# A graph attention kernel on one core: the same operations, ordered by a plan with other sizes and paces of transfers and longer bank copies

## The chip, the core and the metric

One core of a Trainium2 chip. The metric is device time of one execution, in microseconds (us): the median of several runs, on the same data. The engines: PE (TensorE, with PEld for its weight loads), DVE (VectorE), ACT (ScalarE), POOL (GpSimd) and SP (SyncE, which here only issues transfers). SP's transfers make one queue, POOL's another.

## The reference

Input: `x` of 32 x 512 x 512 (32 graphs, 512 nodes, 512 features, f32) and `adj` of 32 x 512 x 512. Per graph, a layer norm and a relu, then two graph attention layers, and the input is added:

```
def gat_layer(x, mask, W, a_src, a_dst, bias, concat):
    xl = (x @ W).reshape(B, N, H, F)
    asrc = einsum('bnhf,hf->bnh', xl, a_src); adst = einsum('bnhf,hf->bnh', xl, a_dst)
    e = leaky_relu(asrc[:, :, None, :] + adst[:, None, :, :], 0.2)
    attn = softmax(where(mask[..., None], e, -1e9), axis=1)
    out = einsum('bsdh,bshf->bdhf', attn, xl)      # heads side by side, or their mean
    return out + bias
h = relu(layernorm(x)); mask = (adj > 0) | eye(N)
h = elu(gat_layer(h, mask, W1, ..., concat=True))      # 4 heads of 256
x = x + gat_layer(h, mask, W2, ..., concat=False)      # 1 head of 512
```

## The kernel before

The kernel writes no loop of instructions in the order in which they run. `tile_gat` adds *jobs* to a `Program`: each has an engine, a cost in us, the keys that it reads and writes, and a function that emits its instructions. A DMA job has also a *size*: the time in us for which the plan takes it to occupy its queue. After all jobs are added, `Program.order` simulates the engines with these costs and so decides each engine's order, and `emit` writes the instructions out in that order. So every instruction stands where the plan put it, and each engine runs its own list in order, waiting by semaphores for data and for buffers that are still read.

How the plan chooses: among the jobs of an engine that are ready, it takes the one with the smallest rank. The ranks come from the table `PLACES` (2374 entries in hundredths of a us): one entry for each job up to the end of the first round (1144), for each of the 470 jobs of a round, and for each job from the last round on (760); a round's entries are used for all rounds between, shifted by the TensorE time of a round (84.5 us by the plan's costs). Transfers are modelled as two wires, SP's and POOL's: a transfer starts `DMA_LEAD` after its issue, lasts its size, and is seen by its readers `DMA_TAIL` later. If both wires are busy, `SHARED` gives the pace of each as a share of its full speed; before, it has two cases, a transposing transfer on SP (of size `TURN`) or any other.

Work is staged so that three graphs are in hand. Round i (lines 1599 to 1650) does, in the order in which the jobs are added:
- the first attention layer's gather of graph i+1, heads 0 and 1 (L1607, `gather1`) and 2 and 3 (L1623), with the softmax numerators of heads 2 and 3 (L1608, L1609, `second`);
- the second layer's scores and numerators of graph i (L1610 `second_layer`, L1611), its gather with the residual (L1632 `residual`, L1633 `gather2`) and the store;
- the first projection of graph i+2 in two halves (L1617 and L1625, `project1`), its masks (L1614 `masks`), its scores (L1619 and L1628 `columns`; L1620, L1621, L1629 and L1630 `first`) and the numerators of heads 0 and 1 (L1626, L1627 `second`);
- load and norm of graph i+3 (L1635, L1636), the second projection of graph i+1 (L1647 `project2`), and the transposing of graph i+3 (L1650 `norm_turn`).

The products use a scheme of seven instead of eight block products (`sevens`): a product's result in a PSUM bank is copied or added out by ACT or DVE (`put`, tile `xl` for the first projection), and one result of each seven is also copied to a second bank by ACT (`FORK`, L1051, `mm<-mm` in the profile); `HALF` is the cost of the halved bank copies of the inner scheme (`step`), `BIAS` that of the gathers' results, `PUT` that of the second gather's.

The scores reach all partitions by way of DRAM (`spread`, L821 on): DVE transposes a small block (L830), SP stores it (`das<-as` or `drr<-rr`, 4 KB), and SP reads it back, repeated over 128 partitions (`as<-das` or `rr<-drr`, 512 KB, for one row pair 256 KB). ACT reads `as` in `first` (`l<-as,z`), DVE reads `rr` in `second` (`p<-rr,z`). The mask is added to the numerators by POOL's transfers (`p<-dm`, two of 512 KB for each head, accumulating), and ACT takes the Exp of the sum (`p<-p,z`).

All instructions are emitted through helpers, so the profile shows ACT's at L498, DVE's at L501, SP's copies at L504, POOL's transfers at L509 and TensorE's at L515, and tells them apart by tiles.

Of the kernel before, what the change touches and what calls it, by code (L numbers as in the profile page):

```python
# [19 lines left out]
P = 128  # L20
# [24 lines left out]
class Banks(Slots):  # L45
# [176 lines left out]
class Program:  # L222
# [9 lines left out]
    DMA_LEAD, DMA_TAIL, AHEAD = {"SP": 0.6, "POOL": 0.75}, {'SP': 1.2, 'POOL': 1.2}, 3.5  # L232
    ALONE = {"SP": 1.0, "POOL": 1.0}
    SHARED = {0: {"SP": 0.44, "POOL": 0.62}, 1: {"SP": 0.3, "POOL": 0.62}}
    TURN = 0.95
    ENGINES = "PE", "ACT", "DVE", "POOL", "SP"

    def __init__(self):
# [44 lines left out]
    def order(self):  # L283
        jobs, rank = self.jobs, self.ranks()
        n = len(jobs)
# [1406 lines left out]
```

## Time and profile before

| | |
|---|---|
| median of 3 runs | 2817.1 us (2813.84 to 2825.34) |
| the profiled execution | 2829.0 us, its span 2827.2 us |
| instructions of the span | 42339 |
| granted TensorE clock, mean | 0.999 |
| transfers | 502.12 MB, mean 178 GB/s |
| share of 16 DMA engines: SP's queue, POOL's queue | 43.1%, 24.8% |
| transfers issued by SP, by POOL | 1296, 318 |

How to read it: the profile is one execution. A group's row gives engine, operation, tiles (written <- read), shape and count, then the busy time, the mean of one in ns, and the idle time of the engine ahead of them with what ended it. A row of a timeline gives the start and the length in us, and in brackets the idle time ahead and its releaser. A row of the waits gives who waited for whom, then the total in us, how often, and the longest. A row of the windows gives the stretch, its length, and the busy time of PE, PEld, DVE, ACT and POOL with their instructions, then the granted clock, the DMA share and GB/s. A wait for several semaphores is put down to the one that came last by the profile.

### The profile page before, as it was taken

To read this page: it belongs to the slowest core of one execution; us is meant where nothing else is said; L and a number is where in the kernel's file an instruction comes from. 1 tells how busy PE (TensorE), PEld (TensorE's weight loads), DVE (VectorE), ACT (ScalarE), POOL (GpSimd) and SP (SyncE) were. 2 spreads that over 40 slices of the span, in tenths; PEclk is the share of its full clock that TensorE was granted. 3 is DMA by queue.
4 is the path that set the end of the run, shared out by engine and by line. 5 is a ranking of instruction groups with operands and counts; after the bars stand their busy time and mean duration, and the time that the engine had idled before them with its cause. 6 is when DMAs were issued, how large, how long until landed. Compare 5 with 4: busy or idle time off the path is not lost.

```text
span 2827.2 us, 42339 instructions
## 1 busy us (share of the span) xinstructions
PE 2766.5 (98%) x12924; PEld 2369.7 (84%) x12924; DVE 2544.8 (90%) x6732; ACT 2223.8 (79%) x4907; POOL 320.0 (11%) x356
## 2 busy tenths in 40 slices
PE   7999999999999999999999999999999999999999
PEld 6688888888888888888888888888888888888877
DVE  8999989999989999999999898899998998989996
ACT  5968888778787787887787877878878788778873
POOL 0110111101111111111011110111110111101110
PEclk9999999999999999999999999999999999999999
DMA  8756866666766767667676667776666766668663
GB/s 232 177 155 165 207 168 179 178 178 180 188 168 172 183 172 197 178 170 194 165 198 172 180 171 182 177 187 183 172 188 163 197 173 170 190 165 198 159 170 104
DMA packets 375863, 502.12 MB, mean 178 GB/s; under 512 B 222804, under 2 KB 227668, under 8 KB 375636
## 3 DMA queue, kind: packets, MB, share of 16 engines
q1 hardware_dynamic: 329844, 332.68, 43.1%
q0 software_dynamic: 45792, 166.74, 24.8%
q8 instruction: 102, 1.67, 0.2%
q14 instruction: 125, 1.02, 0.1%
HBM read 316.41 MB, written 51.31 MB: 130 GB/s over the span
## 4 chain that ended last, share of the span: by engine, by line
PE 37%; DMA 20%; ACT 19%; DVE 15%; issue 3%; SPq 1%; DVEq 0%; ACTq 0%; POOLq 0%
PE mm L515 37%; ACT l L498 10%; DMA as<-das 7%; DVE p L501 6%; DMA rr<-drr 5%; DMA drr<-rr 4%; ACT p L498 3%; DMA x<-in_x_dram 2%; DVE l L501 2%; DVE t L501 2%; ACT xl L498 2%; DVE h L501 1%; ACT mm L498 1%; ACT x L498 1%; DVE xl L501 1%
## 5 line engine op out<-in xcount | busy, mean ns | idle before, releaser
L515 PE MATMUL mm<-w_sb,hs 128*128 128x257 f32 (+3 forms) x2908 | 668.2, 368 | 18.3 <-ACT mm L498 11.8
L515 PEld LDWEIGHTS mm<-w_sb,hs 128*128 128x128 f32 x2908 | 532.4, 190 | 98.0 <-ACT mm L498 16.6
L509 POOL DMA_DIRECT2D p<-dm x314 | 273.8, 902 | 2306.4 <-DVE p L501 1375.1
L515 PE MATMUL mm<-w_sb,ht 128*128 128x258 f32 x2112 | 520.1, 383 | 11.8 <-DVE xl L501 11.6
L515 PE MATMUL mm<-p,xl 128*128 128x258 f32 (+2 forms) x1984 | 511.2, 385 | 2.5 <-ACT h L498 1.1
L515 PE MATMUL mm<-w_sb,h 128*128 128x257 f32 x2056 | 483.1, 380 | 3.5 <-ACT xl L498 2.4
L501 DVE SCALAR_TENSOR_TENSOR p<-rr,z 128x512 f32<-128x512 f32 (+1 forms) x636 | 444.7, 745 | 36.1 <-DMA rr<-drr 36.0
L498 ACT ACTIVATE p<-p,z 128x512 f32<-128x512 f32 (+1 forms) x636 | 425.6, 712 | 43.0 <-DMA p<-dm 30.1
L498 ACT ACTIVATE l<-as,z 128x512 f32<-128x512 f32 x516 | 355.9, 714 | 127.4 <-DMA as<-das 126.9
L515 PEld LDWEIGHTS mm<-w_sb,ht 128*128 128x128 f32 x2112 | 390.6, 191 | 72.5 <-DVE xl L501 20.8
L515 PEld LDWEIGHTS mm<-w_sb,h 128*128 128x128 f32 x2056 | 387.9, 189 | 65.9 <-ACT xl L498 7.1
L515 PEld LDWEIGHTS mm<-p,xl 128*128 128x128 f32 x1984 | 367.3, 190 | 71.9 <-DVE p L501 7.8
L498 ACT ACTIVATE l<-l,low 128x512 f32<-128x512 f32 x516 | 368.6, 718 | 15.1 <-DVE low L501 14.6
L501 DVE CUSTOM_DVE_ANT_1 l<-l,mt 128x512 f32<-128x512 f32 x516 | 349.4, 687 | 23.8 <-ACT l L498 19.6
L498 ACT ACTIVATE xl<-mm 128x258 f32<-128x258 f32 (+2 forms) x748 | 272.0, 377 | 101.0 <-PE mm L515 99.0
L498 ACT ACTIVATE mm<-mm 128x257 f32<-128x257 f32 (+2 forms) x498 | 171.7, 345 | 150.5 <-PE mm L515 150.4
L498 ACT ACTIVATE h<-mm,b_sb 128x256 f32<-128x256 f32 (+1 forms) x504 | 225.3, 472 | 57.3 <-PE mm L515 55.5
L515 PE MATMUL mm<-t,hs 128*128 128x258 f32 (+1 forms) x992 | 246.5, 380 | 0.5 <-DVE t L501 0.5
L515 PEld LDWEIGHTS mm<-t,hs 128*128 128x128 f32 x992 | 186.1, 190 | 30.1 <-DVE xl L501 3.7
L515 PE MATMUL mm<-xl,p 128*128 128x258 f32 (+2 forms) x752 | 195.1, 389 | 3.2 <-DVE h L501 2.1
L498 ACT ACTIVATE xr<-h 128x512 f32<-128x512 f32 x256 | 157.8, 624 | 47.9 <-DVE h L501 45.6
L501 DVE TENSOR_TENSOR xl<-xl,mm 128x258 f32<-128x258 f32 x372 | 153.3, 419 | 29.8 <-PE mm L515 27.9
(137 smaller groups left out, 3727.7 us busy)
## 6 DMA issues: line engine op xcount, KB each, us to landing
p<-dm POOLq DMA_DIRECT2D x314, 512.0 KB, 5.5
rr<-drr SPq DMA_DIRECT2D x159, 512.0 KB
x<-in_x_dram SPq DMA_DIRECT2D x129, 256.0 KB
adj<-in_adj_dram SPq DMA_DIRECT2D x128, 256.0 KB
as<-das SPq DMA_DIRECT2D x64, 512.0 KB
t<-in_x_dram SPq DMA_DIRECT2D x124, 256.0 KB
out_dram<-t SPq DMA_DIRECT2D x124, 256.0 KB
dm<-m SPq DMA_DIRECT2D x64, 256.0 KB
```

Of the source, the lines that this page charges most:

```text
L498: prog.add("ACT", cost, reads, writes, lambda: nc.scalar.activation(*a, **k))
L501: prog.add("DVE", cost, reads, writes, lambda: f(*a, **k))
L509: lambda: nc.gpsimd.dma_start(to, at, accum_op=OP.add), size,
L515: f(*a, **k)
```

## The change

Every job stays, with the same keys, instructions and buffers. Changed are numbers that the plan uses: the table `PLACES` (all 2374 entries), the sizes and paces of the transfers, and some costs of ACT's bank copies. `SHARED` is now looked up by the size of the transfer that SP has under way, with (0.4, 0.6) for sizes that are not listed. Since the plan decides the order, the order of the instructions on PE, DVE, ACT, SP and POOL changes all over, and with it the order in which buffers are taken. The changed kernel's lines stand one lower than those named here.

```
-    DMA_LEAD, DMA_TAIL, AHEAD = {"SP": 0.6, "POOL": 0.75}, {'SP': 1.2, 'POOL': 1.2}, 3.5
-    ALONE = {"SP": 1.0, "POOL": 1.0}
-    SHARED = {0: {"SP": 0.44, "POOL": 0.62}, 1: {"SP": 0.3, "POOL": 0.62}}
-    TURN = 0.95
+    DMA_LEAD, DMA_TAIL, AHEAD = {"SP": 0.45, "POOL": 0.42}, {'SP': 1.2, 'POOL': 1.15}, 3.5
+    SHARED = {0.93: (0.31, 0.7), 0.77: (0.43, 0.71), 2.32: (0.75, 0.31), 1.16: (0.75, 0.31), 1.25: (0.35, 0.57)}
...
-            speed = self.ALONE
+            speed = dict.fromkeys(wires, 1.0)
             if len(busy) == 2:
-                speed = self.SHARED[jobs[wires["SP"][0][0]][4] == self.TURN]
+                speed["SP"], speed["POOL"] = self.SHARED.get(jobs[wires["SP"][0][0]][4], (0.4, 0.6))
...
+    XLOAD, STORE, MASKS, TURN, MASK_OUT, SMALL_ONE = 0.93, 0.77, 2.35, 1.25, 0.8, 0.1
+    ROWS = {4: 1.16, 8: 2.32}
     COPY, ADD, TINY = 0.266, 0.335, 0.08
-    BIAS, FORK, HALF, PUT = 0.37, 0.27, 0.17, 0.4
+    BIAS, FORK, HALF, PUT = 0.365, 0.303, 0.197, 0.394
```

The sizes that are used at the transfers:

| transfer | before | after |
|---|---|---|
| loads of x (also of the residual) and adj, 256 KB | 0.8 | 0.93 |
| loads of W1 | 0.9 | 0.93 |
| store of the output, 256 KB | 0.65 | 0.77 |
| the mask's add, `p<-dm`, 512 KB | 2.3 | 2.35 |
| the mask to DRAM, `dm<-m` | 1.0 | 0.8 |
| transposing transfers | 0.95 | 1.25 |
| the small store of `spread` | 0.2 | 0.1 |
| the repeated read of `spread`, 4 or 8 rows | 0.96, 1.92 | 1.16, 2.32 |

More of the change, by code (lines that the diff above doesn't have):

```diff
@@ L595, in weights1 @@
                     dma(
-                        0.9, (), [("w1", ix, k)], w1_sb[:, ix, k, :, 2:],
+                        XLOAD, (), [("w1", ix, k)], w1_sb[:, ix, k, :, 2:],
                         w1[row : row + P, :].rearrange("p (j c f) -> p c j f", j=H // 2, c=2)[:, c],
@@ L701, in load @@
             xt = xt[:, :D]
-            dma(0.8, (), [xk], xt, x[b, t * P : (t + 1) * P, :])
+            dma(XLOAD, (), [xk], xt, x[b, t * P : (t + 1) * P, :])
             XT[b].append((xk, xt))
@@ L713, in masks @@
                 row = (2 * g + t) * P
-                dma(0.8, (), [ak], a, adj[b, row : row + P, :])
+                dma(XLOAD, (), [ak], a, adj[b, row : row + P, :])
                 dve(
@@ L727, in masks @@
             dma(
-                1.0, every, [mk + (g,)],
+                MASK_OUT, every, [mk + (g,)],
                 md[:, 2 * g : 2 * g + 2].rearrange("p t n -> p (t n)"), m.rearrange("p t n -> p (t n)"),
@@ L736, in masks @@
                 ),
-                prog.TURN,
+                TURN,
             )
@@ L795, in norm_turn @@
                 ),
-                prog.TURN,
+                TURN,
             )
@@ L834, in spread @@
             dma(
-                0.2, [ok], [dk], dr[:k].rearrange("k (b j) -> b k j", j=32),
+                SMALL_ONE, [ok], [dk], dr[:k].rearrange("k (b j) -> b k j", j=32),
                 bass.AP(
@@ L841, in spread @@
             dma(
-                0.24 * rows * n, [dk], [ok], o[:, :rows, : n * P],
+                ROWS[rows * n], [dk], [ok], o[:, :rows, : n * P],
                 bass.AP(tensor=dr.tensor, offset=dr.offset, ap=[[0, P], [n * P, rows], [1, n * P]]),
@@ L961, in second @@
                         accumulate(
-                            2.3, keys + [mk + (us[0] // 2,)], keys,
+                            MASKS, keys + [mk + (us[0] // 2,)], keys,
                             *(t[:, us[0] : us[-1] + 1].rearrange("p t n -> p (t n)") for t in (p, md)),
@@ L1427, in residual @@
             halves = [xk, xk + (0,), xk + (1,)]
-            dma(0.8, [x2_key(b, 0, 0)], halves, xr, x[b, d * P : (d + 1) * P, :])
+            dma(XLOAD, [x2_key(b, 0, 0)], halves, xr, x[b, d * P : (d + 1) * P, :])
             XR[b].append((places[d], xk, xr))
@@ L1484, in put @@
                 upper[u[0]] = -1
-                dma(0.65, [xk, xk + (0,), xk + (1,)], (), out[b, d * P : (d + 1) * P, :], xt)
+                dma(STORE, [xk, xk + (0,), xk + (1,)], (), out[b, d * P : (d + 1) * P, :], xt)
                 place.give(xk)
@@ L1511, in gather2_plain @@
             dve(0.6, [bk, xk], [xk], nc.vector.tensor_add, xr, ps, xr)
-            dma(0.65, [xk], (), out[b, d * P : (d + 1) * P, :], xr)
+            dma(STORE, [xk], (), out[b, d * P : (d + 1) * P, :], xr)
             banks.give(bk)
```

309 rows, old and new, of the table PLACES are left out of this document.

## The prediction

> **What bounds the kernel now.** I read the page's first part, then busy time in three stretches, then TensorE's own waits in the long middle one.
>
> ```profile
> PE 2766.5 (98%) x12924; PEld 2369.7 (84%) x12924; DVE 2544.8 (90%) x6732; ACT 2223.8 (79%) x4907; POOL 320.0 (11%) x356
> ```
> ```profile
> 0.00:87.00 87.00, 70.42 (x316) 57.27 (x317) 74.54 (x294) 52.95 (x121) 8.17 (x14) 1.00 0.79 225
> 87.00:2720.00 2633.00, 2596.88 (x12198) 2235.08 (x12198) 2393.37 (x6251) 2119.61 (x4674) 304.07 (x333) 1.00 0.69 178
> 2720.00:2827.20 107.20, 99.21 (x412) 77.36 (x410) 76.88 (x191) 51.23 (x114) 7.79 (x9) 0.98 0.47 134
> ```
> ```profile
> PE mm L515 <- DVE xl L501: 12.4, 18, 1.4
> PE mm L515 <- ACT mm L498: 11.8, 17, 2.2
> PE mm L515 <- DVE hs L501: 3.5, 6, 1.1
> PE mm L515 <- DVE mm L501: 3.3, 3, 1.7
> PE mm L515 <- ACT xl L498: 2.4, 4, 1.0
> ```
> ```profile
> L515 PE MATMUL mm<-w_sb,ht 128*128 128x258 f32 x2112 | 520.1, 383 | 11.8 <-DVE xl L501 11.6
> ```
> ```profile
> 1542.81 1.69 PE L515 MATMUL mm<-w_sb,hs 128*128 128x258 f32 x7
> ```
>
> TensorE is the bound; in the middle (about 29 rounds) it idles 2633.0 - 2596.9 = 36.1 us. The change keeps every instruction, so only waiting can go. A wait costs a little more than its row shows, because a matmul's record outlasts the start of the next: one is recorded with 383 ns, and 7 in a row take 1.69 us, so starts are (1.69 - 0.38) / 6 = 0.218 us apart and each gap hides about 0.16. (A product of four such matmuls is so 0.87 us of TensorE, one of eight 1.74, one of two half-wide ones 0.22; I use these below.) With that: **A**, waits on DVE's xl, 12.4 + 18 x 0.16 = 15.3 us; **B**, waits on ACT's copies into a bank (FORK), 11.8 + 17 x 0.16 = 14.5; **C**, the three other rows, 9.2 + 13 x 0.16 = 11.3. Together 41.1 us is what the middle can give back, 1.5%. One round shows A and B:
>
> ```profile
> 1513.00:1600.40 87.40, 85.61 (x404) 73.78 (x404) 78.80 (x208) 69.29 (x154) 10.08 (x11) 1.00 0.68 177
> ```
> ```profile
> 1529.03 0.33 SPq L504 DMA_DIRECT2D x<-in_x_dram  x1
> 1529.47 0.37 SPq L504 DMA_DIRECT2D adj<-in_adj_dram  x1
> 1531.08 0.54 SPq L504 DMA_DIRECT2D drr<-rr  x1
> 1531.67 0.51 SPq L504 DMA_DIRECT2D das<-as  x1
> 1532.29 0.66 SPq L504 DMA_DIRECT2D adj<-in_adj_dram  x1
> 1537.34 0.33 SPq L504 DMA_DIRECT2D rr<-drr  x1
> ```
> ```profile
> 1530.85 0.21 DVE L501 STREAM_TRANSPOSE rr<-low 128x32 f32<-128x32 f32 x1
> ...
> 1538.24 0.69 DVE L501 TENSOR_TENSOR ht<-ht 128x512 f32<-128x512 f32 x1
> 1538.84 0.30 DVE L501 TENSOR_TENSOR mm<-mm,f 128x129 f32<-128x129 f32 x1
> ...
> 1539.73 0.30 DVE L501 TENSOR_TENSOR mm<-mm,f 128x129 f32<-128x129 f32 x1
> 1541.87 1.42 DVE L501 SCALAR_TENSOR_TENSOR p<-rr,z 128x512 f32<-128x512 f32 x2 [1.84 <-DMA rr<-drr]
> ```
> ```profile
> 1545.08 0.42 DVE L501 TENSOR_TENSOR xl<-xl,mm 128x258 f32<-128x258 f32 x1
> ...
> 1545.55 1.79 PE L515 MATMUL mm<-w_sb,ht 128*128 128x258 f32 x7 [1.06 <-DVE xl L501]
> ```
>
> This is A. The small row drr (made by first of L1630) is put on SP behind an x load and an adjacency load; the copy rr<-drr that needs it can be issued only at 1537.34, 6.3 us later, behind yet another adjacency load. DVE waits 1.84 us for it, its put of xl ends late at 1545.5, and TensorE loses 1.06 us. DVE is not the bound, but its queue hands the late landing on.
>
> ```profile
> 1553.15 0.52 SPq L504 DMA_DIRECT2D das<-as  x1
> 1553.77 0.39 SPq L504 DMA_DIRECT2D rr<-drr  x1
> 1555.37 0.33 SPq L504 DMA_DIRECT2D t<-in_x_dram  x1
> 1555.80 0.38 SPq L504 DMA_DIRECT2D as<-das  x1
> ```
> ```profile
> 1561.65 1.95 ACT L498 ACTIVATE l<-as,z 128x512 f32<-128x512 f32 x3 [1.05 <-DMA as<-das]
> ```
> ```profile
> 1564.44 1.79 PE L515 MATMUL mm<-w_sb,hs 128*128 128x258 f32 x7 [0.66 <-ACT mm L498]
> ```
>
> This is B: the copy as<-das is issued behind a residual load, ACT stands 1.05 us before its first use, three of these and one more instruction stand ahead of the bank copy, and TensorE waits for that copy. The round's idle time, 87.40 - 85.61 = 1.79 us, is nearly these two gaps, 1.06 + 0.66.
>
> **The change, part by part.** The new sizes and paces move no work by themselves; through the table they give another order, which I read from the built programs. Of one round in the middle:
>
> *A.* On SP the order before is adj, x, adj, drr, das, adj, rr, as, adj; after it is adj, drr, adj, x, das, rr, as, adj, adj. So drr passes two loads and the third adjacency load no longer stands before the copies. On DVE 26 instructions stood between the transpose (1530.85) and the first use of rr, 9.0 us (1531.06 to 1540.03); after it is 33. The net addition is four 512-wide subtractions (0.60 each, as from 1538.24 to 1538.84: the next begins 0.09 before a record of 0.69 ends), an add on rr (1.42 / 2 = 0.7), a 256-wide one (0.42 - 0.09 = 0.33) and two small ones (0.21 - 0.09 = 0.12 each, by the transpose), less one 512-wide statistic (0.60): +3.1 us. The lateness of 1.84 becomes at least 1.2 us of slack (3.1 - 1.84). The issue of rr itself comes 0 to 3.6 us sooner (drr to rr took 6.26 here; das to as, with a copy and a load in between, 2.65); at both ends the wait is gone. The PE product that waits moves four products back too (0.87 each), but the put it needs moves back on DVE as well, so I count nothing for that. A gives back 15.3 us at most; DVE had other small lags in front of the put, and if those alone cause half of it, 8. I take **14**, near the upper end, because the row names the DMA and both edits strike at it.
>
> *B.* On SP the residual load (256 KB) goes behind as<-das. From 1553.77 to 1561.65 a 512 KB, a 256 KB and a 512 KB transfer took 7.9 us; the load's share is 0 us if it was hidden and 7.9 x 256 / 1280 = 1.6 if they run in turn. The transpose that feeds das comes 0 to 1.84 us sooner when A's wait is gone. Between the product whose bank is copied and the product that waits, TensorE had three products (0.87 + 0.22 + 0.22 = 1.31 us), and has 0.22 + 0.87 + 0.87 = 1.96 after, +0.65; but ACT has two more short instructions ahead of the copy, of which the longer kind is
>
> ```profile
> L498 ACT ACTIVATE h<-mm,b_sb 128x256 f32<-128x256 f32 (+1 forms) x504 | 225.3, 472 | 57.3 <-PE mm L515 55.5
> ```
>
> so at most -0.94. The mean loss is 14.5 / 17 = 0.85 us; the gain in hand is -0.3 to 3.4 + 0.65 = 4.1, so B goes by 0 to 14.5. I take **10**: the nearest row, the 1.05 us of ACT, is inside that range, but not where the longest waits (2.2) are.
>
> The Trainium skill, "DMA: Bandwidth & Descriptors", sections "Issuing engines are not separate DMA queues" and "Queues, rings and completion order", says that transfers issued by any engine share the same 16 DMA engines, which take turns between queues packet by packet. It speaks against this part: a copy that passes a load on SP gains at most that load's share, and POOL's adds pay what the copies gain. By the in-turn end above the sum would stand, by the hidden end B would give nothing; no row here shows single turns.
>
> *C.* The second layer's products (L1647) get room: at three places the PE work between a product and the reader of its copy goes from one product of eight (1.74 us) to two, three, and three and a half (3.5, 5.2, 6.1); at one place of the first gather (L1607) from one product of four to three (0.87 to 2.6). Five other places get tight: two products of four (in L1623 four) become one, or one and a small one (1.74 to 0.87 or 1.09), twice in L1607, once in L1623, twice in L1625. C lies between -11.3 and about +11.3 us (as many tight places as now); I take **-6**, since the longest waits belonged to chains that A starts.
>
> Head and tail keep their shape: 16.6 us of idle TensorE at the head, 8.0 at the tail; the first loads and weights stand in another order, which I take at 0, with 4 us either way.
>
> Sum: -14 - 10 - 6 = **-30 us**. The profiled execution took 2829.0 us (span 2827.2), 11.9 above the median of 2817.1, so it would take 2799, and the median becomes **2787 us**.
>
> **Rivals.**
>
> *The gain moves on* (R1). TensorE no longer loses A, reaches the bank copy sooner, and as<-das lands no sooner: B's 17 waits grow by what A gave (15.3 / 29 = 0.5 us a round), and C stays. For it: ACT's waits for as are its longest on a transfer.
>
> ```profile
> ACT l L498 <- DMA as<-das: 124.4, 50, 4.8
> ```
>
> Against it: the chain to das starts behind A's place and moves with it. The time is 2817 - 15 + 29 x 0.4 = about 2813 us.
>
> *POOL's adds become late* (R2, slower). For the second head of L1627, 36 DVE instructions stand before, 25 after, between the last p<-rr and the first use of the finished p; at the round's mean of 78.80 / 208 = 0.38 us that is 13.7 and 9.5 us. The chain there, and ACT's present waits for such adds:
>
> ```profile
> 1506.32 0.86 POOL L509 DMA_DIRECT2D p<-dm  x1 [0.46 <-PE mm L515]
> ```
> ```profile
> p<-dm POOLq DMA_DIRECT2D x314, 512.0 KB, 5.5
> ```
> ```profile
> ACT p L498 <- DMA p<-dm: 29.4, 33, 1.6
> ```
>
> 0.5 us to the issue, 5.5 to the landing, 0.7 for the Exp (the same 512-wide kind as the three of 1561.65): 6.7 of the 9.5, so 2.8 us to spare. If the copies of SP, now packed closer, push the landing past 8.3 us, every microsecond beyond costs a round a microsecond, since the next gather's products read it at once: 29 us in all. From a landing of 9.8 the kernel is slower by over 14 us; at 9.9 it is 29 x 1.6 - 30 = +16, 2833 us. Against it: 5.5 is the median of 314, and ACT's waits for adds are small (29.4 us). The skill's rule of turns is the mechanism of this rival.
>
> *The order does not do what its sizes say* (R3): the plan's landings are no truer than before, old waits go and as long ones come, 2817 us.
>
> **How the numbers follow.** Forecast (A, B and most of C fall; 2762 to 2803): 0.70. R1 0.12, R3 0.09, R2 0.09. A measurement tells about 0.5% (14 us) from no change. Faster by more than that means under 2803: the forecast and 0.02 of R1, 0.72; within it R1's rest and R3, 0.19; slower R2, 0.09. The range: the lower end is 41 us for A, B and C, 4 for the head and tail and 10 for waits of the weight loads that never show as idle matmuls, 2762; the upper end takes in R1 and half of R3, 2816. It leaves out R2, the rest of R3 and a little below.
>
> **What would show it.** A right: no DVE wait for rr<-drr before the p<-rr of L1609, and TensorE's waits on DVE xl fall from 12.4 us to 3 or less. B right: as<-das is issued before the t load, ACT's waits for as fall well below 124.4, TensorE's on ACT mm from 11.8 to 4. C right: the other PE waits halve, and no new row of 5 us stands there. PE's busy time stays at 2766 within 10. Wrong: ACT's waits for p<-dm far above 29.4, or the median landing of p<-dm above 6.5 with DVE waiting for ACT p (R2); TensorE's waits on ACT mm above 12 (R1).

## The result, and the profile after

The changed kernel took **2776.4 us** (median of 4 runs, 2773.0 to 2781.6), the kernel before, beside it, 2816.8 (2813.8 to 2825.3). The ratio is **0.9853**, with a 95% interval of 0.9826 to 0.9880: 40 us faster. In the five-round comparison further below the same kernel gave 0.9833 (0.9818 to 0.9848). The forecast was 30 us. The profiled execution took 2778.1 us (span 2776.3), only 1.8 above its median, while the one of before lay 11.9 above its own; so the two profiles differ by 50.9 us, and some 10 of these are the choice of the execution and not the change.

One correction of what stands above: buffers are bound to jobs when the jobs are added, so a job uses the same buffers in both kernels; only the times change. In the rows after, the helpers' lines stand three lower than before (TensorE's L515 is L512, ACT's L498 is L495, DVE's L501 is L498); in the `x` kernels of the experiments, which carry their order as text, these three are L831, L814 and L817 where the kernel before was edited, and L828, L811 and L814 where the changed one was.

The page's first part, and busy time in the same three stretches (the middle one is cut as before, to begin at 87 us and end 107 us before the end):

```profile
PE 2747.9 (99%) x12924; PEld 2375.5 (86%) x12924; DVE 2561.7 (92%) x6732; ACT 2224.7 (80%) x4907; POOL 321.7 (12%) x356
```
```profile
0.00:87.00 87.00, 72.47 (x307) 58.37 (x308) 72.36 (x285) 49.77 (x113) 7.46 (x13) 0.94 0.78 217
87.00:2669.20 2582.20, 2573.01 (x12186) 2236.20 (x12185) 2408.55 (x6251) 2121.20 (x4676) 305.58 (x333) 1.00 0.68 181
2669.20:2776.30 107.10, 102.39 (x434) 80.93 (x432) 80.82 (x198) 53.69 (x119) 8.71 (x10) 0.99 0.48 138
```

The middle went from 2633.0 us to 2582.2. TensorE's idle time there went from 36.1 to 9.2 us, which is 26.9; the other 23.9 are *busy* time, 2596.9 before and 2573.0 now. About 3 us of these are work, since the cut leaves 12 matmuls fewer in the middle (12186 for 12198). Over the whole span the matmuls are the same 12924, and there busy time fell by 18.6 of the 50.9 us. So a part of the waits was counted as busy.

TensorE's own waits in the middle, all of them (who waited for whom: us in total, times, longest):

```profile
PE mm L512 <- ACT xl L495: 5.9, 11, 1.2
PE mm L512 <- ACT mm L495: 2.0, 4, 1.1
PE mm L512 <- DVE p L498: 0.5, 1, 0.5
PE mm L512 <- ACT f L495: 0.2, 1, 0.2
PE mm L512 <- ACT p L495: 0.2, 1, 0.2
```

The row on DVE xl (A, 12.4 us) is gone, the row on ACT mm (B) went from 11.8 to 2.0, the rows on DVE hs and DVE mm (of C) are gone, and the row on ACT xl grew from 2.4 to 5.9. Where more was lost shows in the waits of the weight loads, which the prediction had only as 10 us at the lower end of its range. Before, then after:

```profile
PEld mm L515 <- DVE xl L501: 25.6, 47, 1.8
PEld mm L515 <- ACT mm L498: 16.6, 22, 2.4
...
PEld mm L515 <- DVE p L501: 7.4, 25, 0.6
PEld mm L515 <- ACT x L498: 7.3, 20, 0.4
PEld mm L515 <- ACT xl L498: 7.1, 13, 1.4
PEld mm L515 <- DVE hs L501: 6.9, 8, 1.5
```
```profile
PEld mm L512 <- ACT xl L495: 8.9, 15, 1.4
...
PEld mm L512 <- ACT mm L495: 4.3, 7, 1.2
PEld mm L512 <- ACT p L495: 2.4, 4, 1.0
```

The 25 waits on DVE p and the 20 on ACT x show in no row of PE of this size. A weight load that comes late can delay its matmul, and while an earlier matmul's record still runs the delay is called busy. But such a wait need not cost its length: of the 47 on DVE xl, 21 (19.1 us) are at A's place, and 22 (3.7 us) at a product of L1623 whose matmuls start only 0.8 us later for it in all 28 rounds. What a place costs is read from the starts of its matmuls; a table of it stands with the third experiment.

The mechanisms of A and B, in the round that matches the one quoted above. SP's queue, then DVE, then SP and ACT for the copy `as`:

```profile
1505.93 0.54 SPq L501 DMA_DIRECT2D drr<-rr  x1
1506.57 0.40 SPq L501 DMA_DIRECT2D adj<-in_adj_dram  x1
1507.01 0.44 SPq L501 DMA_DIRECT2D x<-in_x_dram  x1
1508.18 0.51 SPq L501 DMA_DIRECT2D das<-as  x1
1510.41 0.33 SPq L501 DMA_DIRECT2D rr<-drr  x1
```
```profile
1505.69 0.20 DVE L498 STREAM_TRANSPOSE rr<-low 128x32 f32<-128x32 f32 x1
...
1517.70 1.41 DVE L498 SCALAR_TENSOR_TENSOR p<-rr,z 128x512 f32<-128x512 f32 x2
```
```profile
1528.65 0.52 SPq L501 DMA_DIRECT2D das<-as  x1
1529.26 0.40 SPq L501 DMA_DIRECT2D rr<-drr  x1
1530.96 0.33 SPq L501 DMA_DIRECT2D as<-das  x1
1531.39 0.37 SPq L501 DMA_DIRECT2D t<-in_x_dram  x1
```
```profile
1535.98 1.93 ACT L495 ACTIVATE l<-as,z 128x512 f32<-128x512 f32 x3
```

The small store `drr` now follows its transpose at once, ahead of both loads, and `rr` goes out 4.5 us after it (6.3 before). DVE reaches the first use of `rr` 12.0 us after the transpose (11.0 before, 1.84 of it waiting) and there is no bracket on the row: it does not wait. The copy `as` goes out ahead of the residual load, and ACT uses it 5.0 us after its issue, unheld; before it was used after 5.9 us, and ACT had stood for it. ACT's and DVE's waits for these transfers, and for POOL's adds, in the middle stretch:

```profile
ACT l L495 <- DMA as<-das: 7.9, 13, 1.4
ACT p L495 <- DMA p<-dm: 5.1, 7, 1.5
```
```profile
DVE p L498 <- DMA rr<-drr: 0.6, 2, 0.4
```
```profile
p<-dm POOLq DMA_DIRECT2D x314, 512.0 KB, 5.0
```

They were 124.4 us for `as`, 29.4 for the adds and 34.7 for `rr`; the adds' median landing was 5.5 us. The waits for both queues fell.

### The profile page after: what moved, and what is told of

Its sections match the earlier page's. It is cut to its first block, busy times and chain, and to the rows that moved or that the text cites. A ratio compares the mean times of both kernels' runs of the same rounds, so it can differ in the third digit from the quotient of the medians.

```text
span 2776.3 us, 42499 instructions
## 1 busy us (share of the span) xinstructions
PE 2747.9 (99%) x12924; PEld 2375.5 (86%) x12924; DVE 2561.7 (92%) x6732; ACT 2224.7 (80%) x4907; POOL 321.7 (12%) x356
## 5 line engine op out<-in xcount | busy, mean ns | idle before, releaser
L512 PE MATMUL mm<-w_sb,hs 128*128 128x257 f32 (+3 forms) x2908 | 675.8, 368 | 12.8 <-ACT xl L495 5.9
L512 PEld LDWEIGHTS mm<-w_sb,hs 128*128 128x128 f32 x2908 | 540.1, 190 | 93.3 <-ACT xl L495 8.9
L512 PE MATMUL mm<-w_sb,ht 128*128 128x258 f32 x2112 | 522.8, 382 | 0.1
L512 PE MATMUL mm<-p,xl 128*128 128x258 f32 (+1 forms) x1984 | 493.1, 383 | 1.5 <-ACT mm L495 0.8
L512 PE MATMUL mm<-w_sb,h 128*128 128x257 f32 x2056 | 487.2, 379 | 0.2 <-ACT mm L495 0.2
L498 DVE SCALAR_TENSOR_TENSOR p<-rr,z 128x512 f32<-128x512 f32 (+1 forms) x636 | 447.4, 742 | 4.6 <-DMA rr<-drr 4.4
L512 PEld LDWEIGHTS mm<-w_sb,ht 128*128 128x128 f32 x2112 | 394.5, 190 | 58.0 <-issue 0.7
L495 ACT ACTIVATE p<-p,z 128x512 f32<-128x512 f32 (+1 forms) x636 | 428.2, 713 | 19.6 <-DVE p L498 13.0
L512 PEld LDWEIGHTS mm<-w_sb,h 128*128 128x128 f32 x2056 | 389.3, 189 | 58.2 <-ACT mm L495 0.6
L512 PEld LDWEIGHTS mm<-p,xl 128*128 128x128 f32 x1984 | 365.1, 190 | 61.2 <-issue 5.5
L495 ACT ACTIVATE l<-l,low 128x512 f32<-128x512 f32 x516 | 369.7, 717 | 1.9 <-DVE low L498 1.6
L495 ACT ACTIVATE l<-as,z 128x512 f32<-128x512 f32 x516 | 353.2, 715 | 14.6 <-DMA as<-das 14.3
L498 DVE CUSTOM_DVE_ANT_1 l<-l,mt 128x512 f32<-128x512 f32 x516 | 345.3, 688 | 18.1 <-ACT l L495 12.7
L495 ACT ACTIVATE xl<-mm 128x258 f32<-128x258 f32 (+2 forms) x748 | 274.2, 376 | 81.5 <-PE mm L512 80.2
L495 ACT ACTIVATE mm<-mm 128x257 f32<-128x257 f32 (+2 forms) x498 | 169.8, 345 | 203.3 <-PE mm L512 108.4
L495 ACT ACTIVATE h<-mm,b_sb 128x256 f32<-128x256 f32 (+1 forms) x504 | 227.8, 473 | 121.5 <-PE mm L512 121.0
L512 PE MATMUL mm<-t,hs 128*128 128x258 f32 (+1 forms) x992 | 254.7, 380 | 0.0
L512 PEld LDWEIGHTS mm<-t,hs 128*128 128x128 f32 x992 | 183.6, 190 | 24.0 <-DVE xl L498 0.4
L495 ACT ACTIVATE xr<-h 128x512 f32<-128x512 f32 x256 | 159.7, 625 | 45.5 <-DVE h L498 42.8
L512 PE MATMUL mm<-xl,p 128*128 128x258 f32 (+3 forms) x752 | 190.0, 388 | 0.0
L498 DVE TENSOR_TENSOR xl<-xl,mm 128x258 f32<-128x258 f32 x372 | 155.7, 420 | 36.2 <-PE mm L512 31.7
```

What stands on the lines that cost most here:

```text
L495: prog.add("ACT", cost, reads, writes, lambda: nc.scalar.activation(*a, **k))
L498: prog.add("DVE", cost, reads, writes, lambda: f(*a, **k))
L512: f(*a, **k)
```

## The experiments

The plan's output can be edited by itself: each `x` kernel below is the kernel before or the changed one with its own order written into the program and a few instructions moved, in all 28 steady rounds alike; every instruction and buffer stays. Products are named by their number among the round's 470 jobs; "a round" is the mean gap between the end of one product and the start of the next, worked out from the starts of the matmuls of 25 rounds. A's place is product 158 of L1617, B's is product 278 of L1625 (L1624 in the changed kernel). Ratios are to the kernel before on the same chip, five rounds if nothing else is said.

The first four runs told two theories apart: **Q**, that SP's queue order (A and B as the prediction has them) made the gain, and **W**, that the room in DVE's and TensorE's orders did.

### A alone, in the kernel before (x1_rows_first)

```
 SP: adj
-    x
-    adj
     drr<-rr
+    adj
+    x
     das<-as
-    adj
     rr<-drr
     as<-das
+    adj
     adj
```


> The kernel before, with three moves on SP alone in every round: drr ahead of the x load and the second adjacency load, the third adjacency load behind rr and as. Theory Q (the queue order on SP is what made A): DVE's waits for rr fall from 34.7 us to under 10, TensorE's waits on DVE xl from 12.4 to under 5, time down 8 to 15 us, 2802 to 2809. Theory W (the room that DVE's and TensorE's new orders give is what counts; SP alone does little): time within 4 us of before, TensorE's waits on DVE xl over 9.

Measured: 0.9953 (0.9938 to 0.9968), 13 us. TensorE's waits:

```profile
PE mm L831 <- DVE mm L817: 7.5, 12, 1.4
PE mm L831 <- ACT mm L814: 6.6, 15, 0.9
PE mm L831 <- ACT xl L814: 5.2, 7, 1.3
...
PE mm L831 <- DVE xl L817: 0.3, 1, 0.3
```

DVE's waits for `rr` fell from 34.7 to 9.0 us and A's row is gone with nothing but SP's order changed. A part of the loss came up again at product 131 of L1617 (DVE mm): 0.14 us a round before, 0.42 here. By the trace, this is the price of the move. The second adjacency load now goes out behind `drr`; DVE makes the mask from it 4.6 us after its issue (6.6 before, both means of 28 rounds), and waits for it more often, before and here:

```profile
DVE m L501 <- DMA adj<-in_adj_dram: 5.5, 3, 2.3
```
```profile
DVE m L817 <- DMA adj<-in_adj_dram: 10.8, 17, 1.6
```

Each of the 17 rounds with such a wait has a gap of about the same length ahead of product 131, 3.5 us later; in the other rounds the gap is 0.05 us in the mean. The changed kernel has this part of SP's order too, but its DVE makes that mask 8.2 us after the issue, and does not wait.

### B alone, in the kernel before (x2_as_first)

```
 SP: das<-as
     rr<-drr
-    t (residual load)
     as<-das
+    t (residual load)
```


> The kernel before, with one move on SP alone in every round: the residual load that stood ahead of as<-das goes behind it. Theory Q: ACT's waits for as fall from 124.4 by 25 to 45 us (1 to 1.6 us in each of 28 rounds), TensorE's waits on ACT mm from 11.8 to under 6, time down 5 to 10 us, 2807 to 2812. Theory W: time within 4 us of before, waits on ACT mm over 9.

Measured: 0.9948 (0.9934 to 0.9961), 15 us. TensorE's row on ACT mm fell from 11.8 to 1.9 us, and A's stayed the longest:

```profile
PE mm L831 <- DVE xl L817: 9.2, 14, 1.8
PE mm L831 <- DVE hs L817: 3.7, 7, 0.9
PE mm L831 <- DVE mm L817: 3.4, 3, 1.6
```

ACT's waits for `as` fell only from 124.4 to 110.0 us, by less than the 25 to 45 of theory Q. Most of that row was therefore not what TensorE waited for; the 14 us that went are about what the kernel gained.

### A and B, in the kernel before (x3_both)

Both edits above.

> The kernel before with the moves of both. Theory Q: the sum of the two, 15 to 25 us down, 2792 to 2802, over half of the whole change. Theory W: at most 8 us down, 2809 or more; most of the change's 40 us then lies in the other engines' orders.

Measured: 0.9911 (0.9896 to 0.9926), 25 us, nearly the sum of the two. ACT's waits for `as` are still 106.4 us and DVE's for `rr` 10.3; the changed kernel's 7.9 and 0.6 come from its other orders.

Where the time lies can be counted from the traces: a product is late by as much as its matmuls start later than in an unbroken row (0.217 us from start to start for 258 columns, 0.111 for 129). Summed over the 28 rounds of each profiled execution, in us:

| product | before | x1 | x2 | x3 | changed |
|---|---|---|---|---|---|
| 158 (A) | 16.2 | 0.0 | 14.9 | 0.0 | 0.0 |
| 278 (B) | 16.4 | 9.6 | 3.5 | 1.5 | 0.0 |
| 131 | 3.5 | 12.7 | 3.7 | 12.5 | 0.2 |
| 38, 442 and 14 | 14.8 | 18.0 | 12.1 | 15.0 | 1.1 |
| 214 and 232 | 4.7 | 1.8 | 5.0 | 1.5 | 0.0 |
| 280 | 0.8 | 0.0 | 0.0 | 0.0 | 9.8 |
| all of the round | 59.8 | 46.1 | 45.1 | 34.5 | 14.9 |

The last row falls by 13.7, 14.7 and 25.3 us for the three edits, as the measured times do (13, 15 and 25).

### A and B undone, in the changed kernel (x6_both_behind)

```
 SP: adj                          SP: das<-as
+    adj                              rr<-drr
+    x                           +    t (residual load)
     drr<-rr                          as<-das
-    adj                         -    t (residual load)
-    x
     das<-as
```


> The changed kernel with SP's order put back at the two places: the second adjacency load and the x load ahead of drr again, the residual load ahead of as<-das again; all other engines as changed. Theory Q: 10 to 25 us up, 2786 to 2801, DVE's waits for rr and ACT's for as come back. Theory W: within 4 us of the changed kernel, since the room on DVE and TensorE covers later landings.

Measured: 0.9935 (0.9918 to 0.9952), so 0.8 to 1.0% is lost again. The third adjacency load stays behind `rr` and `as<-das`, so A is undone in two of its three moves. The time is lost at one place, product 280 (1.07 us a round):

```profile
PE mm L828 <- ACT xl L811: 25.7, 29, 1.7
PE mm L828 <- DVE xl L814: 3.6, 1, 3.6
PE mm L828 <- ACT mm L811: 0.9, 2, 0.7
```

ACT's waits for `as` rise from 7.9 to 30.1 us, while DVE's for `rr` are 3.4 us, still a tenth of what the kernel before has. Q holds for about 25 of the 40 us; W holds for the rest, and for `rr` in the changed kernel DVE's order is cover enough. The next runs split this and asked where the rest lies. Their theories: **S**, the time lies at a few places, each with a spare of its own; **G**, the plan as a whole gives it, and what one place gives back turns up at the next.

### A undone, B undone, each in the changed kernel (x4_rows_behind, x5_as_behind)

x4 has the left half of the edit above, x5 the right half.

> The changed kernel with one part of SP's order undone in every round: the third x load and the second adj load stand ahead of drr again, the residual load stays behind as<-das. Theory S (the time lies at a few places, each with a spare of its own; DVE's new order gives the rows' put so much spare that SP's order there no longer counts): TensorE's waits on DVE xl stay at 0, the time is that of the changed kernel within 0.2%, 2773 to 2782. Theory G (the whole plan gives the time, any place in SP's order that is moved back costs its share): half of the 22 us that undoing both cost, 2786 to 2792.

> The changed kernel with the other part of SP's order undone: the residual load stands ahead of as<-das again, drr stays ahead of the x and adj loads. Theory S: ACT's waits on as<-das go from 7.9 to about 30 and TensorE's on ACT xl from 5.9 to about 25, as in the run with both undone; 2798 to 2806, so that this part alone carries nearly all of the 22 us. Theory G: half of it, 2786 to 2792.

Measured, on one chip on which the kernel before took 2830 us, so that the ratios count and not the microseconds expected: x4 0.9845 (0.9830 to 0.9860), not to be told from the changed kernel; x5 0.9904 (0.9887 to 0.9921), 0.5 to 0.7% above it and 16 us above x4. That is nearer to S than to G's two halves. In x4, DVE's wait for `rr` is 6.7 us in all; in x5 it is product 280 again, close behind B's place, that waits, on the copy `xl` behind ACT's first uses of `as`:

```profile
PE mm L828 <- ACT xl L811: 28.6, 27, 1.7
PE mm L828 <- ACT mm L811: 2.7, 3, 1.4
```

### The wait that is left, taken away by hand (x7_copy_sooner, x9_elu_later, after_again)

In the changed kernel the longest gap left is ahead of product 280 of L1624: 0.31 us a round, on the bank copy that ACT puts behind its first three uses of `as` and an elu. The edit puts it ahead of the third of these uses and of the elu, 1.1 us sooner (the expectations speak of three instructions; it passes two).

```
 ACT: first, first                 x9 beside that:
+     put xl (for 280)            -     elu
      first                             h<-mm, fork, step copies
      elu                         +     elu
-     put xl (for 280)
```


> The changed kernel with one ACT instruction moved in every round: the bank copy of step at L1624 that product 280 of the round waits for (put xl, 0.37 us) stands ahead of three first (two Exp and an elu) instead of behind them, 0.6 to 1.9 us sooner. Nothing else moves. Theory S: the wait of product 280 (0.31 us a round in the changed kernel, 13 of 28 rounds above 0.1 us) goes, TensorE's row on ACT xl falls from 5.9 to below 1.5, and the time falls by 28 x 0.31 = 9 us less what comes up behind, to 2766 to 2772. Theory G: the wait moves on to another place of the round, and the time stays within 0.15%, 2772 to 2780.

> The run with the bank copy moved ahead of three ACT instructions (x7) and, beside that, one elu of L1622 behind the copies that products 278 and 268 need; its own user on DVE started 3.2 us after it, so that it can stand 1.1 us later. In x7 the wait of product 280 had gone and 0.47 us a round had come up at product 268 instead, behind those copies. Theory S: with the elu out of the way both waits are below 0.1 us a round; 28 x (0.68 - 0.2) = 13 us less than x7, 0.45 to 0.6% less than the unedited kernel beside it. Theory G: the wait comes up at yet another place; within 0.2% of x7.

> The changed kernel itself, unedited, so that the two kernels with small moves stand beside it on one chip. Both theories: 0.9853 of the kernel before, within 0.2%; the wait of product 280 again at about 0.31 us a round.

Measured: x7 0.9831 (0.9815 to 0.9847), after_again 0.9833 (0.9818 to 0.9848), x9 0.9857 (0.9837 to 0.9876). TensorE's longest rows in the unedited kernel, in x7 and in x9:

```profile
PE mm L512 <- ACT xl L495: 8.0, 19, 0.7
PE mm L512 <- ACT mm L495: 1.4, 2, 1.2
```
```profile
PE mm L828 <- ACT mm L811: 8.7, 18, 1.4
PE mm L828 <- ACT xl L811: 0.9, 1, 0.9
```
```profile
PE mm L828 <- ACT mm L811: 7.2, 21, 1.5
PE mm L828 <- DVE xl L814: 1.9, 2, 1.6
```

The wait only walks: from product 280 (0.42 us a round in after_again) to 268 in x7 (0.47), to 272 in x9 (0.44), each behind the next ACT copy of the same stretch. S had 9 and 13 us to gain here and is wrong; G holds. It points to ACT's whole list from the landing of `as` to the last of these copies, though no run changes that alone. Neither version beats the changed kernel.

### The rest, by hand, in the kernel before (x8_three_places, x10_one_place)

Products 131, 38, 14 and 442 make 0.84 of the 1.04 us a round that x3 still loses. x8 moves what each waits for: on DVE the scaling in `step` (job 128) ahead of three others, two more DVE instructions ahead of one, one copy of ACT ahead of two. x10 keeps only the first, and by one place.

```
 DVE, x8 (on top of x3)      DVE, x10 (on top of x3)
     op of L1623                  op of L1623
+    scaling (job 128)            mask product
     mask product                 elu
     elu                     +    scaling (job 128)
     op of step 3                 op of step 3
-    scaling (job 128)       -    scaling (job 128)
```


> The kernel before with both SP edits (x3) and, beside them, four small moves that the changed kernel's order also has or that its late places ask for: on DVE the scaling in step at L1617 ahead of one mask product, one elu and one op of step 3 (1.5 us sooner), one subtraction at L1607 ahead of another (0.6 us sooner), one op at L1607 ahead of cols (0.15 us sooner), and on ACT one bank copy at L1647 ahead of two Exp (1.2 us sooner). Theory S: the waits of the products 131, 38, 14 and 442 (0.42, 0.20, 0.13 and 0.09 us a round in x3, 0.84 of its 1.04) fall below 0.2 together, and the time falls by 28 x 0.7 = 19 us from 2799.7 to 2778 to 2785, which is most of what the changed kernel has beyond x3. Theory G: they come back at other places, and the time stays above 2791.

> The kernel before with both SP edits (x3) and one DVE instruction moved one place: the scaling in step at L1617 stands ahead of one op of step 3 (0.6 us sooner; its input was there 0.9 to 1.2 us before it started). Moved three places (x8) it came 0.27 us ahead of its input and DVE stood. Theory S: the wait of product 131 (0.42 us a round in x3) falls below 0.1, and the time falls by 28 x 0.35 = 10 us, from 0.9911 to 0.9875 of the kernel before. Theory G: DVE, 92% busy in this stretch, gives it back at the next product that waits for it; 0.990 to 0.992.

Measured: x8 **1.0011** (1.0002 to 1.0020), which gives back the 25 us of x3 and more; x10 0.9895 (0.9878 to 0.9911), 0.16% below x3 with intervals that overlap. In x8 the waits of TensorE and of DVE have new first rows:

```profile
PE mm L831 <- DVE ht L817: 17.9, 28, 0.9
```
```profile
DVE mm L817 <- PE mm L831: 20.7, 26, 1.4
```

The scaling, 1.5 us sooner, now came ahead of its own input, so that DVE stood, 20.7 us in all or 0.8 us each time (not the 0.27 that the expectation of x10 has); an op of step 3 queued behind it was late, and product 154, which reads that op's result, waited 0.82 us in every round. In x10 the gap of product 131 fell nearly as forecast (0.42 to 0.12), and the products just behind it, 148, 154 and 158, took back 0.20. DVE's waits for adjacency loads were still 11.6 us there: x8 and x10 move an instruction that stands behind the waiting mask, and not the mask. Theory S is wrong here too; x10 is between the two.

### The sizes without the table (e2_new_costs, three rounds)

The diff above without `PLACES`: the new sizes, paces and costs, the table of before.

> The sizes and paces of the changed kernel with the table of places of the kernel before: half of the change alone. The table holds due times that were found under the old sizes, and each job is still put by the order of the due times as the model runs. Theory C (sizes and table fit only together): instructions change places all over the round, and the time is well above that of the kernel before, 2860 to 3050. Theory D (the better sizes help by themselves, the table is the fine part): below the kernel before, 2790 to 2810.

Measured: 1.0812 (1.0791 to 1.0833), 3058 us; theory C, a little above its range. The longest rows of TensorE are new ones, and POOL's adds land after a median of 6.1 us:

```profile
PE mm L513 <- DVE hs L499: 37.2, 30, 3.5
PE mm L513 <- ACT xl L496: 32.3, 34, 2.6
PE mm L513 <- ACT mm L496: 27.2, 44, 1.8
```

The new sizes bring nothing by themselves. The table's entries are due times that were found under one set of costs, and under other costs the same entries give another order. The other half of the change, the new table with the old sizes, was not run.

## Why the prediction was right, and where it was not

- **The bound, and that only waits can go**: right that only waits went, too low as a bound. "Together 41.1 us is what the middle can give back" was counted from idle time; by the starts of the matmuls the 28 rounds alone were late by 59.8 us before and by 14.9 after. The three stretches were cut to equal lengths, so they do not show what head and tail gave; their idle time went from 24.6 to 19.2 us.
- **A, taken at 14 us**: right in place and cause; that the size came out too is in part luck. The SP half alone gave 13 us (x1), DVE's waits for `rr` fell, and the row on DVE xl is gone. But these 13 are 23.0 us won at the products of A and B less what came up elsewhere, 9.2 of it at product 131, behind the adjacency load that had to stand back. The prediction put no price on that load. It added SP's gain and DVE's room; for `rr`, the runs show that either alone does most of it (x1 from the one side, x4, with two of the three moves undone, from the other). For the load that stands back DVE's room is needed: by the traces, it is what the changed kernel has and x1 has not.
- **B, taken at 10**: right in cause, low in size. Moving one load behind `as<-das` gave 15 us (x2), all of what the row with its hidden part had (14.5); product 278 itself was late by 16.4 us before, by 3.5 in x2 and not at all in the changed kernel. The prediction shrank it since the longest waits looked longer than the load could explain. Its sign was only half right: `as` is issued ahead of the load and ACT mm fell to 2.0 as forecast; but ACT's waits for `as` falling far below 124.4 was not the mark of B, for x2 took B away with 110.0 left.
- **C, taken at -6**: this step was the furthest off, in its size. Beyond the two edits on SP (0.9911) the changed kernel has another 0.6 to 0.8% (0.9853 and 0.9833), 16 to 22 us; the table has 19.6 (34.5 to 14.9), of which 12.3 lie at product 131, most of it the price that x3 pays and the changed kernel does not. "C lies between -11.3 and about +11.3 us" was counted from the three short rows of TensorE. Their products (38, 131 and 442; to 38 and 442 the prediction had given room) lost 13.1 us of lateness from before to after. Products 14, 214 and 232, whose weight loads waited for ACT x, DVE p and ACT h, lost another 8.6, and they were in no term, only as 10 us at the lower end of the range. Product 280 came up with 9.0. The net is some -12. And "PE's busy time stays at 2766 within 10" was wrong: it fell by 18.6 us over the span, since short gaps count as busy. The mark for C was half right: the three rows fell from 9.2 us to 5.9, because ACT xl grew to 5.9 while the others went, and that is a new row of over 5 us.
- **0.16 us hidden by each wait**: too little as the price of all that is hidden. The visible waits and this term give 41.1 - 11.7 = 29.4 us (8.8 us and 18 waits are left), which is the 30 forecast; the profiles differ by 50.9. A gap shorter than the overlap of two records leaves no idle time at all: in the middle there were 138 gaps of 0.05 to 0.165 us before, 13.4 us together, and 47 after, 4.7 us.
- **R1, the gain moves on**: not for A and B as a whole. It did happen where a place was mended by hand (x7, x9, x10), at the next instructions of the same engine. Product 131 in x1 is another matter: there the load that was moved behind is late.
- **R2, POOL's adds become late**: no. Their median landing went from 5.5 to 5.0 us, far from 8.3, and ACT's waits for them from 29.4 to 5.1. The Trainium skill ("DMA: Bandwidth & Descriptors", "Queues, rings and completion order") says that each DMA engine takes turns between the queues that have work for it, and from this rule the prediction had the adds pay for what the copies gain. No such price shows: with A's SP edit alone the landing was 5.1, with B's 5.6. No run here shows single turns; what the runs show is that the sequence within SP's queue counted. The price fell within that queue, on the adjacency load (10.8 us of DVE's waits in x1); the residual load, which comes later by B's edit, has no row of waits.
- **R3, the order does not do what its sizes say**: no for the change as a whole. Whether the landings of the plan are truer was not measured; the new sizes under the old table made the kernel 8% slower (e2).

What stays open: which moves on the other engines make the 16 to 22 us beyond A and B. The traces say where the time lies: products 131, 38, 442 and 14 are late by 27.5 us in x3 and by 1.3 in the changed kernel, which loses 9.8 at product 280. For 131 they also name the cause, the later mask on DVE, but no run moves that mask alone. Four places of x3 were tried by hand, and none gave the time. Whole engines' orders, but for POOL's, cannot be exchanged singly between the two kernels, since by the jobs' keys they would wait for each other in a circle.

## What to carry to other kernels

On a queue of transfers in strict order, ask of each small store or copy that starts a chain what big load stands ahead of it, and then who reads that load and when: two such moves gave 25 us here, and by the traces one of them would have given more if the reader of the load had stood later. When TensorE is nearly full, read the starts of its matmuls and not only its idle time: 18.6 of the 50.9 us between the two profiles were recorded as busy. The waits of the weight loads point to such places, but can be longer than what they cost. And a hand move of one microsecond in a list that is 92% busy can give the loss to the next instruction in line (x10) or make a bigger one (x8); look in the trace whether its input is there by then, and expect to have to move the whole stretch.

## What the hardware showed beside that

- The same 12924 matmuls were recorded with 2747.9 us of busy time in the changed kernel, 2766.5 before and 2773.6 in x8, at a clock of 0.998 to 0.999 each, by the order alone; busy time is not work. (In e2 it was 2851.2, but there the clock was lower too.) The weight loads' busy time moved less and the other way, 2375.5, 2369.7 and 2369.9 us. The Trainium skill, "Perfetto Trace Analysis", section "Identifying the Most-Contended Engine", says that the busy share of matmuls is a bad measure of closeness to the limit and names that of the weight loads instead, beside MFU, the operations done as a share of the peak; these rows agree.
- The granted clock was 0.998 to 1.000 over the span of every profiled execution but one; in e2, where TensorE was busy for 93% of the span, it was 0.977. Over the first 87 us it was 0.94 in the changed kernel and 1.00 in the one before, with nearly the same busy time there (72.5 and 70.4 us), so the sum of idle time alone does not set it. No run here says what does.
